# Spreading a 7-of-8 block product over four heads, two pools of PSUM banks for its parts, and an earlier fixed order

## The chip, the cores and the metric

The kernel runs on one core of one Trainium2 chip. The metric is device time in microseconds of one execution, all of it included: two layers of a transformer-like block from input in HBM to output in HBM. Less is better. Everything is computed in fp32.

## The reference

Four rows (B = 4) of 512 tokens with 512 channels. Two layers add to a residual `x`, and each branch is preceded by a gate made of a two-sided recurrence (WKV) over a side input:

```python
x = x + _L0_attn_ref(_L0_cond_ref(x, f, f, ...), ...)      # Mamba2
x = x + _L0_ffn_ref(_L0_cond2_ref(x, f, f, ...), ...)      # 8 experts, top 2
x = x + _L1_attn_ref(_L1_cond_ref(x, f, f, ...), ...)      # attention, where the change is
x = x + _L1_ffn_ref(_L1_cond2_ref(x, f, f, ...), ...)      # gated FFN
```

The attention, with 4 key groups of 4 heads each (16 heads of 128 channels):

```python
q = einsum('bsh,he->bse', x, w_q).reshape(b, 512, 4, 4, 128)
k, v = split(einsum('bsh,he->bse', x, w_kv), 2)            # one k and v for each group
scores = einsum('bqgpd,bkgd->bgqpk', q, k) * 128 ** -0.5   # causal
probs = softmax(scores)
ctx = einsum('bgqpk,bkgd->bqgpd', probs, v).reshape(b, 512, 2048)
return einsum('bse,eh->bsh', ctx, w_dense)
```

A gate is `sigmoid(x)` times a quotient of exponentially decaying sums over the tokens, forward and backward, of `exp(k)` and `exp(k) * v`. The sums depend on the side input alone, not on `x`, so gates can be made at any time before they are applied.

## The kernel before

**Stages.** Mamba2 and the first gates; the experts (37 rounds of 128 tokens each, every round three products of 8 TensorE instructions of 512 columns); attention; the gated FFN. The program is written out in Python, and a tile framework orders each engine's instructions by priority and by what is ready in its own model. Where the text says `with after(engine)`, an instruction is queued on that engine behind the last one written before it.

**Gates.** `make_gates` (L354) is a generator over pairs of channel blocks: for layer 1 there are 16 pairs, two for each of eight gates. `pump(n)` (L387) makes n larger steps of it, six to a pair, and `nudge()` (L392) one small step. After each expert round, the function `more` (L1566) calls `pump(1 + moe.i % 2)`; in attention each score block calls `nudge`. A pair is four forward scans (L259), four backward scans (L265), six products on VectorE (L276 to L280), a reciprocal by Relu, Ln and Exp on ScalarE (L316 and the lines behind it) and three last VectorE products (L322 to L333).

**Heads.** The main loop runs over `heads_`, that is (g, b, i): group, row, head. For head n it makes the queries of the next head, runs `scores` of this one, then `ahead(n)`, which makes queries, keys and values of later heads, then `settle()`, which multiplies the probabilities of three heads ago with the values (`context`), and then `dense_parts(n)`.

- `scores` (L1801): four score products `psc` (L1821) into "mm" banks, for the four blocks of 128 query tokens, each with a mask (L1824) and a row maximum (L1826) on VectorE and an exponential on ScalarE (L128). Then the probabilities are normalized, transposed in 32 x 32 blocks on VectorE (L1811), written to HBM by four DMAs on GpSimd's queue (L1850), and read back a head later as `pT` (L1868, in `collect`).
- `context` (L1873): `pctx` (L1895) into an "acc" bank; ScalarE copies it to `cx` (L1906).
- When four heads of (g, b) are through, their contexts are multiplied with the group's slice of `w_dense` and added to `x[b]`. `dense` (L1909) does it in four pieces of 8 instructions of 512 columns. `dense7` (L1930) does it as a 2 x 2 block product by Winograd's form, with seven half products in place of eight: seven `part`s of 8 instructions of 256 columns. It needs sums of weights (`dense_sums`, L1633, on GpSimd, queued by `to_sum`) and sums of contexts (L1959 to L1967, on VectorE, in place). Each part ends with two VectorE additions (L1952) to one to four blocks of `x[b]`. It is used from (1, 0) to (3, 0), nine times.
- `parts` holds the generator of the block at work; `dense_parts(n)` takes n parts of it.

**PSUM.** Eight banks: four "mm" (scores, keys, values), two "tp" (queries, transposes), two "acc" (contexts and dense parts).

**Order.** `even[0]` is true from head (0, 3, 1) to (3, 3, 1). There `in_turn()` makes TensorE run scores, contexts, queries and dense products as they are written; `scores` leaves normalizing to ScalarE (`late`, L1845) and skips one of its four nudges; and dense products are spread over the next heads. Outside it the framework orders TensorE freely, normalizing is on VectorE (L1836, L1837), and `settle` runs the whole dense product at once.

**GpSimd** also makes the sums of the query weights (`pair_weights`, L1518 to L1521), in the heads (g, 3, 0) and (g, 3, 2) of groups 1 and 2, and likewise at the end of group 0.

Of the kernel before, what the change touches and what calls it, by code (L numbers as in the profile page):

```python
# [14 lines left out]
ALU = mybir.AluOpType  # L15
# [68 lines left out]
def block_kernel(ctx: ExitStack, tc: tile.TileContext, a: dict, out: bass.AP):  # L84
# [1476 lines left out]
    with tc.tile_pool(name="moe_w2", bufs=1, reuse_waits="tile") as wm:  # L1561
# [4 lines left out]
        def more(limit):  # L1566
            while moe.i < min(limit, moe.known):
                moe.round()
                if moe.i < ALWAYS - NT + 1:
                    with after(nc.vector, nc.scalar):  # L1570
                        send()
                        pump(1 + moe.i % 2)

# [37 lines left out]
    with att as ph:  # L1611
# [318 lines left out]
        def dense7(u):  # L1930
            a11, a12, a22 = (dense_w[u.g, *v] for v in ((0, 0), (0, 1), (1, 1)))
            s1, s2, s3, s4 = dense_s[u.g]
            lo, hi = slice(0, HT), slice(HT, T)
# [3 lines left out]

            def part(w, xs, q0, q1, step=1, op=ALU.add):
                po = ps_acc("pd")
                with in_turn():  # L1940
# [12 lines left out]

            part(a11, b11, 0, 4)
            if last:
                load_dense(u.g + 1, 0, 0)
            t2 = gq.tile([P, 2, HT], F32, tag="t2", name="t2")
            for c in range(2):
                nc.vector.tensor_tensor(b11[c], b12[c], b11[c], ALU.subtract)  # L1959
                nc.vector.tensor_tensor(t2[:, c], b22[c], b11[c], ALU.subtract)  # L1960
                nc.vector.tensor_tensor(b12[c], b22[c], b12[c], ALU.subtract)
            yield True
            part(a12, b21, 0, 1)
            if last:
# [3 lines left out]
            yield True  # L1968
            part(s4, b22, 1, 2)
            yield True  # L1970
            part(s2, [t2[:, c] for c in range(2)], 1, 4)
            yield True
            part(s3, b12, 2, 4)
            if last:
                load_dense(u.g + 1, 1, 0)
            yield True
            part(a22, b21, 2, 3, op=ALU.subtract)
            if last:
                load_dense(u.g + 1, 1, 1)
                to_sum.append(u.g + 1)  # L1980
            yield True
            part(s1, b11, 1, 4, 2)
            yield None
# [4 lines left out]
        def settle():  # L1988

            old, done = held.pop(0)  # L1990
            context(old, done)
            if len(old.ctxT) == HPG:
                assert not parts
                parts.append((dense7 if seven(old) else dense)(old))
                sevens[0] = seven(old)
                if not even[0]:
                    dense_parts(NC)

        def dense_parts(n):
            while parts and n:  # L2000
                n -= 1
                if next(parts[0], None) is None:
                    parts.pop()

# [28 lines left out]
        def ahead(n):  # L2033
# [3 lines left out]
            if i % 2:  # L2037
                if heads_[n + 1 : n + 2] and heads_[n + 1] in making_q:
                    lead(n + 1)
                if n + 3 < len(heads_):  # L2040
                    lead(n + 3)
            elif n + 2 < len(heads_):
                lead(n + 2)
            s = n + 4 - i
            if i >= 2 and s < len(heads_):
                with after(nc.tensor):
# [10 lines left out]
        look_ahead(1, (0, 1))  # L2057
        groups, making_q, qs, pairs_w, parts, loading, sevens = {}, {}, {}, {}, [], [], [False]
        numbers = iter(range(GROUPS * B * HPG))
        ready, held = begin(0), []  # L2060
        for n, (g, b, i) in enumerate(heads_):
            u, qT = ready
            even[0] = (0, B - 1, 1) <= (g, b, i) < (GROUPS - 1, B - 1, 2)
            if g == 0 and i == 0 and b + 1 < B:
# [39 lines left out]
            if len(held) > 3:  # L2104
                settle()
            twice = sevens[0] and i != 2 or g == GROUPS - 1 and (b, i) >= (2, 2)
            dense_parts(2 if twice else 1)
            if (g, b, i) == (GROUPS - 1, 2, 1):
# [227 lines left out]
```

## Time and profile before

| | |
|---|---|
| time, median of 3 runs | 2237.92 us (2235.61 to 2240.21) |
| the profiled execution | 2231.51 us, span 2229.8 us, granted TensorE clock 0.979 |
| busy | PE 2101.0, DVE 1619.4, ACT 1035.7, POOL 512.0 us |
| experts with gates of layer 1 | about 744 to 1062 us |
| attention, group 0 | about 1113 to 1328 us, its last heads from 1236 |
| attention, 7-of-8 products | about 1428 to 1890 us |
| last heads | about 1890 to 1982 us, then the FFN |

Times are from one profiled execution, in us from the first instruction. PE is TensorE's multiplications, PEld its weight loads, DVE VectorE, ACT ScalarE, POOL GpSimd, SP the engine that issues most DMAs. A row of waits names the waiting engine, tile and line, then what it waited for, the sum, the number and the longest. In a row of the timeline stand start, length, engine, line, operation, tiles, shape and number, and in brackets the engine's idle time before it and what ended it. A wait for several things is put down to the last by the profile; where the named one was long done, it was another. Two rows of one tile's matmuls start one behind the other, so the distance of their starts is TensorE's cost of the first.

### The profile page before, as it was taken

Reading aid. Unit: us, or ns where it says so; the run is one execution under the profiler, and the core shown is the slowest. Engines: PE = TensorE matmul, PEld = TensorE weight load, DVE = VectorE, ACT = ScalarE, POOL = GpSimd, SP = SyncE. Lnnn points to the kernel's source line nnn. Section 1 sums busy time; section 2 is a strip of 40 time slices with the busy share of each in tenths; the row PEclk is TensorE's granted clock in tenths of the full one; section 3 lists DMA queues with packets and bytes.
Section 4 is the critical chain, followed back from the end, with each engine's and each line's share of the span. In section 5 each row is a group of like instructions: output and inputs, shape, how many; then the busy total and the mean of one; then the engine's idle time right before and its main releaser. Section 6 shows DMA issues by size and latency. Waiting matters only on the chain.

```text
span 2229.8 us, 25287 instructions
## 1 busy us (share of the span) xinstructions
PE 2101.0 (94%) x8074; PEld 1321.0 (59%) x8074; DVE 1619.4 (73%) x3026; ACT 1035.7 (46%) x2071; POOL 512.0 (23%) x684
## 2 busy tenths in 40 slices
PE   4879999999999999999988989999999999999998
PEld 2545565555665444444444546677777777568887
DVE  8699989999752566676479865788989788655332
ACT  4476676675832134333255434454545454532221
POOL 4022232422222111212233322213232223100000
PEclk9989999999999999999989999999999999999999
DMA  7542251442424458987577766666767676541100
GB/s 255 186 142 77 96 168 67 140 139 66 176 76 147 156 187 293 385 290 274 208 273 259 224 206 192 213 221 206 232 203 226 195 214 194 154 164 38 38 20 20
DMA packets 128619, 391.30 MB, mean 175 GB/s; under 512 B 15904, under 2 KB 37280, under 8 KB 117024
## 3 DMA queue, kind: packets, MB, share of 16 engines
q1 hardware_dynamic: 93088, 249.86, 32.5%
q0 software_dynamic: 33088, 135.55, 19.5%
q10 hardware_dynamic: 2304, 4.20, 0.5%
q8 instruction: 67, 1.10, 0.2%
q14 instruction: 72, 0.59, 0.1%
HBM read 363.34 MB, written 116.39 MB: 215 GB/s over the span
## 4 chain that ended last, share of the span: by engine, by line
PE 38%; DVE 7%; ACT 2%; DMA 2%; issue 1%; SPq 0%; POOL 0%; DVEq 0%; POOLq 0%; ACTq 0%
PE pctx L1895 5%; PE pq L1764 5%; PE pd L1914 4%; PE pd L1943 4%; PE psc L1821 4%; PE pv L1724 2%; PE pk L1713 2%; PE pfo L2166 2%; PE pfo L2165 2%; PE pfg L2165 2%; PE pfg L2166 2%; PE pfu L2165 2%; PE pfu L2166 2%; DMA pT<-turned 1%; PE pq L1741 1%; DVE nmax L1826 1%
## 5 line engine op out<-in xcount | busy, mean ns | idle before, releaser
L128 ACT ACTIVATE pr<-psc,nmax 128x128 f32<-128x128 f32 (+3 forms) x256 | 133.6, 524 | 286.5 <-DVE nmax L1826 285.4
L1850 POOL DMA_DIRECT2D turned<-turned x248 | 135.6, 553 | 565.8 <-DVE turned L1811 453.1
L1821 PE MATMUL psc<-kT,qT 128*128 128x128 f32 (+3 forms) x512 | 158.6, 449 | 17.6 <-ACT pr L128 17.6
L1895 PE MATMUL pctx<-pT,v 128*128 128x512 f32 (+3 forms) x512 | 152.3, 442 | 9.8 <-DMA pT<-turned 9.1
L1057 PE MATMUL pc<-h,wxb 128*128 128x512 f32 x320 | 144.0, 604 | 5.0 <-DVE h L406 4.0
L1895 PEld LDWEIGHTS pctx<-pT,v 128*128 128x128 f32 x512 | 97.3, 194 | 75.6 <-issue 53.3
L847 PE MATMUL po<-w,yT 128*128 128x512 f32 x296 | 134.1, 593 | 0.2 <-ACT yT L840 0.2
L814 PE MATMUL pg<-w,hT 128*128 128x512 f32 x296 | 133.9, 593 | 0.0
L825 PE MATMUL pn<-w,hT 128*128 128x512 f32 x296 | 133.3, 592 | 0.0
L1811 DVE STREAM_TRANSPOSE turned<-pr 128x128 f32<-128x128 f32 x248 | 119.7, 499 | 12.4 <-ACT pr L1845 6.7
L1821 PEld LDWEIGHTS psc<-kT,qT 128*128 128x128 f32 x512 | 87.7, 194 | 58.5 <-ACT pr L128 28.1
L1826 DVE TENSOR_REDUCE nmax<-psc 128x1 f32<-128x128 f32 (+3 forms) x256 | 118.4, 482 | 0.6
L1128 PE MATMUL pz<-wzt,h 128*128 128x512 f32 x256 | 116.9, 606 | 0.3 <-ACT st L1229 0.3
L1276 PE MATMUL po<-wot,yT 128*128 128x512 f32 x256 | 114.2, 600 | 0.0
L1057 PEld LDWEIGHTS pc<-h,wxb 128*128 128x128 f32 x320 | 60.6, 194 | 76.2 <-issue 71.7
L1845 ACT ACTIVATE pr<-pr,rsum 128x128 f32<-128x128 f32 x196 | 94.0, 551 | 11.9 <-DVE rsum L1843 11.9
L1764 PE MATMUL pq<-ht,wq 128*128 128x256 f32 x384 | 98.5, 379 | 0.0
L1914 PE MATMUL pd<-cx,wd 128*128 128x512 f32 x224 | 98.5, 592 | 0.0
L1952 DVE TENSOR_TENSOR xr<-xr,pd 128x256 f32<-128x256 f32 (+3 forms) x126 | 80.0, 679 | 20.7 <-PE pd L1943 20.1
L1171 ACT ACTIVATE lm<-lm,cs 128x128 f32<-128x128 f32 x256 | 81.8, 390 | 22.8 <-DMA lm<-cs 22.7
L825 PEld LDWEIGHTS pn<-w,hT 128*128 128x128 f32 x296 | 54.8, 190 | 61.7 <-issue 61.7
L814 PEld LDWEIGHTS pg<-w,hT 128*128 128x128 f32 x296 | 54.6, 190 | 60.8 <-issue 60.7
(384 smaller groups left out, 4780.7 us busy)
## 6 DMA issues: line engine op xcount, KB each, us to landing
w<-in_w1x SPq DMA_DIRECT2D x76, 1024.0 KB
turned<-turned POOLq DMA_DIRECT2D x248, 208.0 KB, 3.8
pT<-turned POOLq DMA_DIRECT2D x62, 832.0 KB, 7.4
w<-in_w2x SPq DMA_DIRECT2D x38, 1024.0 KB
wb<-in_b1x SPq DMA_DIRECT2D x38, 512.0 KB
lm<-cs SPq DMA_DIRECT2D x32, 512.0 KB
kt<-in_fT SPq DMA_DIRECT2D x62, 256.0 KB
ek<-ek SPq DMA_DIRECT2D x62, 256.0 KB
```

Source lines behind the costliest of these rows:

```text
L814: nc.tensor.matmul(pg, lhsT=hT[:, k, :], rhs=self.w1[s][0][:, k, :], start=(k == 0), stop=(k == NC - 1))
L825: nc.tensor.matmul(pn, lhsT=hT[:, k, :], rhs=self.w1[s][1][:, k, :], start=(k == 0), stop=(k == NC - 1))
L847: nc.tensor.matmul(po, lhsT=yT[:, j, :], rhs=self.w2[s][:, j, :], start=(j == 0), stop=(j == NI - 1))
L1057: nc.tensor.matmul(pc, lhsT=wxb[:, k, m * P : (m + 1) * P], rhs=h[:, k, :], start=(k == 0), stop=(k == NC - 1),)
L1764: nc.tensor.matmul(out_, lhsT=w[:, c], rhs=xs[:, c], start=(c == 0), stop=(c == 1))
L1821: nc.tensor.matmul(psc[:, :n], lhsT=qT[:, qi * P : n], rhs=u.kT[:, :n], start=True, stop=True)
L1826: nc.vector.tensor_reduce(nmax, psc[:, :n], AX.X, ALU.max, negate=True)
L1850: nc.gpsimd.dma_start(out=d[:, :, r].rearrange("c i s -> i c s"), in_=blocks[r * SQ : (r + 1) * SQ].rearrange("i c k j -> i c (k j)"),)
L1895: nc.tensor.matmul(pctx[:, kj * P :].rearrange("p (q r j) -> p q r j", r=QUAD, j=SQ), lhsT=u.v[:, kj, :], rhs=pT[:, :, 4 * kj : 10 + kj : ...
L1914: nc.tensor.matmul(po, lhsT=dense_w[u.g, m % 2, i // 2][:, i % 2, m // 2], rhs=u.ctxT[i], start=(i == 0), stop=(i == HPG - 1),)
L2165: nc.tensor.matmul(out_, lhsT=w, rhs=xs[0], start=first_, stop=False)
L2166: nc.tensor.matmul(out_, lhsT=w, rhs=xs[1], start=False, stop=last_)
```

## The change

It edits five places.

1. After an expert round `pump` makes two steps, where it made one and two in turn.
2. `dense7`: the six first context sums move from behind part a11 to ahead of part a12, a head later. Parts s4, s3 and s1 take a bank of the "mm" pool, the others stay in "acc". `to_sum` is filled after the last part, not before it.
3. `parts` may hold two blocks; the older one is worked off first.
4. How many parts follow a head: with 7-of-8 products, it was one after a block's third head (i = 2) and two after the others; from (1, 2, 0) on it is one after i = 3 and two after the others. As the first block before that takes one part in each of two heads, the last part (s1) of each block lags into the head in which the next block's a11 comes.
5. `even` is true from (0, 2, 2), three heads sooner. Guards in `ahead` keep these heads from making queries, keys and values early for group 0.

```diff
-                        pump(1 + moe.i % 2)
+                        pump(2)
...
-            def part(w, xs, q0, q1, step=1, op=ALU.add):
-                po = ps_acc("pd")
+            def part(bank, w, xs, q0, q1, step=1, op=ALU.add):
+                po = bank("pd")
...
-            part(a11, b11, 0, 4)
+            part(ps_acc, a11, b11, 0, 4)
             if last:
                 load_dense(u.g + 1, 0, 0)
+            yield True
             t2 = gq.tile([P, 2, HT], F32, tag="t2", name="t2")
             for c in range(2):
                 nc.vector.tensor_tensor(b11[c], b12[c], b11[c], ALU.subtract)
                 nc.vector.tensor_tensor(t2[:, c], b22[c], b11[c], ALU.subtract)
                 nc.vector.tensor_tensor(b12[c], b22[c], b12[c], ALU.subtract)
-            yield True
-            part(a12, b21, 0, 1)
+            part(ps_acc, a12, b21, 0, 1)
...
-            part(s4, b22, 1, 2)
+            s1, s2, s3, s4 = dense_s[u.g]
+            part(ps_mm, s4, b22, 1, 2)
             yield True
-            part(s2, [t2[:, c] for c in range(2)], 1, 4)
+            part(ps_acc, s2, [t2[:, c] for c in range(2)], 1, 4)
             yield True
-            part(s3, b12, 2, 4)
+            part(ps_mm, s3, b12, 2, 4)
...
-            part(a22, b21, 2, 3, op=ALU.subtract)
+            part(ps_acc, a22, b21, 2, 3, op=ALU.subtract)
             if last:
                 load_dense(u.g + 1, 1, 1)
+            yield True
+            part(ps_mm, s1, b11, 1, 4, 2)
+            if last:
                 to_sum.append(u.g + 1)
-            yield True
-            part(s1, b11, 1, 4, 2)
             yield None
...
-                assert not parts
                 parts.append((dense7 if seven(old) else dense)(old))
-                sevens[0] = seven(old)
...
-                    parts.pop()
+                    parts.pop(0)
...
-                if n + 3 < len(heads_):
+                if n + 3 < len(heads_) and heads_[n + 3][0]:
                     lead(n + 3)
-            elif n + 2 < len(heads_):
+            elif n + 2 < len(heads_) and heads_[n + 2][0]:
                 lead(n + 2)
             s = n + 4 - i
-            if i >= 2 and s < len(heads_):
+            if i >= 2 and s < len(heads_) and heads_[s][:2] > (0, B - 1):
...
-            even[0] = (0, B - 1, 1) <= (g, b, i) < (GROUPS - 1, B - 1, 2)
+            even[0] = (0, B - 2, 2) <= (g, b, i) < (GROUPS - 1, B - 1, 2)
...
-            twice = sevens[0] and i != 2 or g == GROUPS - 1 and (b, i) >= (2, 2)
-            dense_parts(2 if twice else 1)
+            if (1, 2, 0) <= (g, b, i) < (GROUPS - 1, 2, 2):
+                dense_parts(1 if i == 3 else 2)
+            else:
+                dense_parts(3 if (g, b, i) == (GROUPS - 1, 2, 2) else 2 if g == GROUPS - 1 and b >= 2 else 1)
```

More of the change, by code (lines that the diff above doesn't have):

```diff
@@ L1931, in dense7 @@
             a11, a12, a22 = (dense_w[u.g, *v] for v in ((0, 0), (0, 1), (1, 1)))
-            s1, s2, s3, s4 = dense_s[u.g]
             lo, hi = slice(0, HT), slice(HT, T)
@@ L2057, in block_kernel @@
         look_ahead(1, (0, 1))
-        groups, making_q, qs, pairs_w, parts, loading, sevens = {}, {}, {}, {}, [], [], [False]
+        groups, making_q, qs, pairs_w, parts, loading = {}, {}, {}, {}, [], []
         numbers = iter(range(GROUPS * B * HPG))
```

## The prediction

> **What bounds the kernel now.** I read the page first, then busy time by stage, then TensorE's waits stage by stage, then single moments in the timeline.
>
> From the page, the share of each engine, and the group of VectorE additions that empty the product's banks:
>
> ```profile
> PE 2101.0 (94%) x8074; PEld 1321.0 (59%) x8074; DVE 1619.4 (73%) x3026; ACT 1035.7 (46%) x2071; POOL 512.0 (23%) x684
> ...
> L1952 DVE TENSOR_TENSOR xr<-xr,pd 128x256 f32<-128x256 f32 (+3 forms) x126 | 80.0, 679 | 20.7 <-PE pd L1943 20.1
> ```
>
> TensorE is the bound. The change removes no matmul, so it can only win TensorE's idle time. Busy time by stage (stretch, length, PE, PEld, DVE, ACT, POOL, granted clock, DMA share, GB/s):
>
> ```profile
> 744.00:1062.00 318.00, 312.77 (x910) 149.91 (x909) 210.62 (x307) 111.78 (x155) 60.89 (x54) 1.00 0.75 266
> ...
> 1236.00:1328.00 92.00, 84.00 (x267) 45.63 (x266) 70.72 (x154) 39.31 (x89) 30.32 (x46) 0.94 0.66 213
> ...
> 1428.00:1890.00 462.00, 449.37 (x1973) 340.87 (x1972) 397.90 (x890) 221.81 (x557) 125.50 (x211) 1.00 0.67 211
> 1890.00:1982.00 92.00, 87.49 (x294) 49.85 (x293) 48.08 (x117) 37.85 (x88) 11.46 (x21) 0.98 0.58 189
> ```
>
> The four stages that the change touches: experts (5.2 us idle), the last heads of group 0 (8.0), the heads with 7-of-8 products (12.6), the last heads (4.5): 30.4 us is the ceiling, plus matmuls slowed after a wait. VectorE is at 86% in the third stage (397.9 of 462) and at 66% among the experts.
>
> TensorE's waits in the 7-of-8 stage, whole:
>
> ```profile
> PE pv L1724 <- ACT pr L128: 4.6, 3, 2.3
> PE pd L1943 <- ACT cx L1906: 4.4, 5, 1.7
> PE pctx L1895 <- DMA pT<-turned: 3.6, 2, 2.0
> ```
>
> In group 0's last heads and in the last heads of all, the timeline shows one wait each that matters, both on TensorE:
>
> ```profile
> 1320.76 4.50 PE L1895 MATMUL pctx<-pT,v 128*128 128x512 f32 x8 [5.59 <-DMA pT<-turned]
> ```
>
> ```profile
> 1935.38 0.49 PE L1821 MATMUL psc<-kT,qT 128*128 128x128 f32 x2 [2.55 <-ACT pr L128]
> ```
>
> The same context product takes 2.32 us elsewhere and 4.50 here: 2.2 us more at a low granted clock (0.94 over the stage), so this one wait costs 7.8.
>
> **The change part by part.**
>
> *Second bank pool.* Within a head, the context product takes one of two "acc" banks, the first part the other, and the second part must wait until ScalarE has copied the context away. That is the 4.4 us row: five such waits out of 27 heads with two parts. With one part of each pair in an "mm" bank, nothing waits for that copy. Against it: the mm bank must be free again for the next head's fourth score product. After the mm part come the acc part (8 matmuls of 0.216 = 1.7 us) and three score products (1.3 us): 3.0 us of cover. The additions take 2 x 0.68 = 1.4 us at most, and the page's row has VectorE waiting for the part (20.1 us), not behind it, in 21 of 63 parts. Where VectorE lags by over 1.6 us the rest is paid, and the exponentials queue behind it. In the 1515.8 case it lagged by 1 us. I take -4 (between -4.4 and +3, 27 heads by 0.1).
>
> *Order of parts and sums.* A finished block's four heads had 1, 2, 2, 2 parts; now, with the last one lagging into the next block, 2, 1, 2, 2. The third head (with the key product, 3.4 us) grows from 12.1 to 13.8 us of TensorE, the fourth (with the value product, 3.6 us) shrinks by 1.7. TensorE's total is unchanged. The eight 0.42 us subtractions now come a head after the part whose operands they overwrite, so VectorE's 17.0 us of idle before them (waiting for that part) goes. This is what made scores late before the value product: subtractions (2.5 us) and two 1.2 us additions stood ahead of the first masks. But the worst of it is GpSimd:
>
> ```profile
> 1639.68 3.30 DVE L1959 TENSOR_TENSOR cx<-cx 128x256 f32<-128x256 f32 x1 [1.58 <-PE pd L1943]
> ...
> 1643.35 2.35 DVE L1952 TENSOR_TENSOR xr<-xr,pd 128x1024 f32<-128x1024 f32 x2
> ```
>
> A subtraction of 0.42 us takes 3.30 while three weight sums of 1.28 us run on GpSimd. `to_sum` moves one head later too, so for groups 2 and 3 both sides move together and meet again, only group 1 comes free (its weight sums stay). What waits for it then is the s4 part, some 1.3 us later in its head than the value product. The waits of 4.6 us become about 2.5: -2 (bounds -4.6, +2).
>
> Here a rule speaks against the change. The Trainium skill ("SBUF — State Buffer", Who interferes with whom) says that a VectorE instruction with two SBUF inputs fully blocks behind a GpSimd instruction that reads SBUF. The 3.30 us row agrees. By that rule the subtractions of block 1, now at the start of head (g, 3, 0), meet the query weights' sums there; blocked in full in both groups, the sum below would be 3.4 us smaller, -8.1 in place of -11.5.
>
> By rows: the query sums run 0.73 + 0.72 + 0.72 us from 1507.13, 0.9 us after that head's scores begin, and already stretched a scan from 1.2 to 2.3 us. In two places this puts up to 2.2 us on VectorE, whose transposes feed the context two heads on, just where the 3.6 us row waits (1524.98 and 1727.86): I take +1 (bounds -3.6, +4.4).
>
> *Fixed order three heads sooner.* From (0, 2, 2) the scores, contexts, queries and product go to TensorE as written, normalizing moves to ScalarE, and the product of block (0, 1) is spread over four heads. Now it runs in one piece, 1282.6 to 1296.3, between the third and fourth score product of head (0, 2, 3), so that head's transposes end only at 1301, GpSimd writes them then, does three query sums, and reads pT at 1314.6: the 5.59 us wait. Spread, that softmax ends some 10 us sooner and 3.4 us parts lie between. In (1, 3, 1), where this spreading already holds, the same spot waits 1.7. So 7.8 becomes about 2: -5.5. What it may cost: scores (0, 2, 2) queue behind the context (0, 1, 2), scores (0, 2, 3) behind the keys, values and queries of row 3. Before, row 3's keys began at 1269.6, ahead of those scores, so the order is nearly the same. At worst two new waits of 5.6: bounds -7.8, +6. ScalarE takes 1.9 us more in each of three heads, at 43% load.
>
> *Two gate steps after each expert round.* Steps per round go from 1.5 to 2 in some 28 rounds: 14 steps. Gate pairs end every 44.6 us there, four rounds, six steps: 2.3 pairs more. Each is about 17.8 us of VectorE (four scans of 1.21, four of 1.27, six ops of 0.69, three of 1.2) and 8 of ScalarE. VectorE's load there goes from 66% to 79%. The load DMAs (six of 256 KB per pair, on SP's queue among the expert weights) add 4% to a stage whose DMA share is 0.75; counting packets against issues, the 1 MB weight loads land 1.4 to 7.6 us after issue and are used some 16 us after it, so I cost that at nothing; if the cover is gone each late load stalls a round by its lateness. What can hurt is ScalarE: a pair's reciprocal (1.15 + 1.15 + 1.06 us, two table loads of 1.28) stands before the next tanh:
>
> ```profile
> 799.66 0.63 PE L838 MATMUL pyt<-ident,u 128*128 128x128 f32 x4 [1.41 <-DVE u L832]
> ```
>
> Two of the six pairs there cost 1.4 us so. With 8 or 9 pairs at another phase: 3 or 4 of them, and routing's 2.0 us wait a little longer: +2 (bounds -3 if none, +10 if all).
>
> What this buys: pairs take some 90 us each in attention (the last four end at 1685, 1777, 1868 and 1940), so the last one ends some 210 us sooner, about 1730. The 2.55 us wait above, with 0.79 and 0.47 beside it, stands behind that pair's reciprocal on ScalarE (1933.83, 1935.21). Of 3.8 us: -3 (bounds -3.8, 0).
>
> *At nothing:* the guards in `ahead` keep group 0 from making queries early, as before; `load_dense` stays with its parts (one of four pieces comes a head later, still several heads ahead of use); the GpSimd weight sums (4 x 1.27 us) come one head later, as does their reader.
>
> Sum: -4 - 2 + 1 - 5.5 + 2 - 3 = -11.5, say -12. The profiled execution took 2231.51 (span 2229.8): 2219.5. The median of the three runs, 2237.92, lies 6.4 above it; with the same gain, 2226.
>
> **The rivals.**
>
> *Waits only move (15%).* The bank wait becomes a wait of the fourth score product, the pT chain binds again: only half of group 0's gain and the end remain, about -5: 2233. For: VectorE stays at 86%. Against: it waits for the parts.
>
> *Fixed order stalls (10%).* Two more waits of 5.6 in the three heads eat the rest: -12 + 5.5 + 6 = about 0: 2238. For: 5.59 was seen in the first fixed heads. Against: it had a bulk product ahead of it.
>
> *Slower: the experts pay (15%).* ScalarE and VectorE come late for each round's tanh. Each such round costs 1.4 us; beyond 9 rounds (12 / 1.4) above today's two the gain is gone, and 20 of 28 give +25 - 12: 2251. For: 79% VectorE, in-order. Against: rounds with two steps exist already, 14 of them, and from 879 to 1058 TensorE has no wait.
>
> *Chain gains as summed: 60%.*
>
> **How the numbers follow.** About 0.2% (4.5 us) can be told from no change. Faster: 0.60 and half of the first rival, 0.68. Same: the other half and half of the second, 0.13. Slower: the rest, 0.19. The low end adds 12 us to the gain (all pv and pctx waits gone, no new expert stall): 2214. The high end takes in the second rival and part of the third, leaving out some 10%: 2245.
>
> **What would show it.** Right: in the 7-of-8 stage no pd wait for cx; the 5.59 us wait at 2 or less; no gate operation after about 1750 and the last psc waits gone; gate scans denser among the experts with TensorE's waits there under 8 us; block (0, 1)'s product in four pieces. Wrong: psc waiting for pd's additions, new waits before queries in (0, 2, 3), or many pyt waits before 1062.

## The result and the profile after

The changed kernel took 2250.28 us (median of 7 runs, 2243.01 to 2253.60), the kernel before 2237.92 beside it: ratio 1.0055 (95% interval 1.0039 to 1.0071), so about 12 us slower. The forecast was 2226 us, in a range from 2214 to 2245: wrong in sign and out of the range. The profiled execution took 2251.86 us (span 2249.9, clock 0.970). It lies 20.1 us above the profiled span before: that execution lay 6.4 us below its median and the one after 1.6 above.

Lines of changed code have moved: `part` multiplies at L1942 and adds at L1951. The page after, the engines' shares and the additions that empty the product's banks:

```profile
PE 2120.3 (94%) x8074; PEld 1333.3 (59%) x8074; DVE 1605.4 (71%) x3005; ACT 1051.3 (47%) x2089; POOL 516.8 (23%) x684
...
L1951 DVE TENSOR_TENSOR xr<-xr,pd 128x256 f32<-128x256 f32 (+3 forms) x126 | 80.2, 678 | 51.9 <-PE pd L1942 51.8
```

VectorE now waits 51.8 us for parts in place of 20.1: the additions did come free of what stood ahead of them. TensorE's idle time is no smaller (129.6 us of the span after, 128.8 before). By stretches, each from the start of one matmul to that of another:

| stretch | before | after | measured | forecast |
|---|---|---|---|---|
| start to expert round 6 (nothing edited) | 744.0 | 747.1 | +3.1 | 0 |
| rounds 6 to 10, with the second routing | 50.7 | 57.0 | +6.3 | +2 with the next |
| round 10 to the first keys (pk) | 318.9 | 329.8 | +10.9 | |
| first keys to the first score product of (0, 2, 0) | 124.5 | 128.8 | +4.3 | 0 |
| on to the first of (0, 3, 3) | 104.2 | 99.6 | -4.6 | -5.5 |
| on to the first of (1, 1, 2) | 86.4 | 86.4 | 0 | 0 |
| on to the first of (3, 2, 2), the "7-of-8 stage" below | 454.0 | 450.2 | -3.8 | -5 |
| on to the FFN, "the end" below | 99.5 | 103.2 | +3.7 | -3 |
| FFN | 247.6 | 247.9 | +0.3 | 0 |

(124.5 and 128.8 are each two stretches added. The expectations name the marks of the 7-of-8 stage as third scores; its length is the same.) A length is that of one profiled execution. Over the runs, the stretch before round 6, which nobody edited, took 744.0 to 751.9 us, and rounds 6 to 10 with the old steps 50.7 or 52.4. Of the -3.8, 1.7 is the lagging part of the last block: its 8 matmuls run behind (3, 2, 2) now and are in the +3.7.

The loss lies mostly where two gate steps follow a round. The +4.3 behind it comes with the steps too (+6.1 with the steps alone, -0.6 with all the rest of the change). It is not idle time (TensorE idled 15.2 us there, 16.7 before): the granted clock was lower, 0.88 from the first score product on where it was 0.92 before. What lowered it was not taken apart. Busy time of three of the changed stages after (experts, last heads of group 0, 7-of-8 products; same columns as before):

```profile
747.00:1084.00 337.00, 320.26 (x914) 153.01 (x913) 243.19 (x345) 135.44 (x182) 63.39 (x55) 0.98 0.74 269
1262.00:1348.00 86.00, 79.84 (x262) 45.01 (x261) 59.53 (x131) 44.58 (x99) 29.47 (x46) 0.96 0.69 220
1448.00:1906.00 458.00, 448.26 (x1964) 341.12 (x1963) 373.50 (x868) 214.59 (x548) 125.71 (x211) 0.99 0.65 206
```

Among the experts VectorE rose to 72% (243.19 of 337), not to 79%, and TensorE idled 16.7 of 337 us. Its waits there, all of them:

```profile
PE po L847 <- ACT yT L840: 4.5, 4, 1.5
PE ptok L606 <- DVE os L600: 4.4, 1, 4.4
PE pyt L838 <- DVE u L832: 4.0, 2, 2.4
PE pg L814 <- DMA w<-in_w1x: 2.7, 3, 1.5
PE pidx L691 <- DVE of L688: 0.6, 1, 0.6
PE pn L825 <- DMA w<-in_w1x: 0.4, 1, 0.4
```

They sum to 16.6 us; before there were three rows (pyt 2.8, pidx 2.0, ptok 0.4; 5.2 us). The waits cost more than their length: taking each matmul's distance to the next start, less that of an undisturbed one of its shape (0.429 us for 512 columns), the excess from round 6 to the first keys went from 12.5 to 29.6 us. These 17.1 us are the two stretches' +17.2. What comes on top of the waits is a lower clock behind the two longest: behind the 4.42 us of ptok the granted clock was 0.50 from 766 to 770 us, behind a 2.42 us wait of pyt 0.50 from 833.4 to 836.4. Behind the 1.51 us of po at 1029.95 it stayed at 1.00.

How each arises is seen in the timeline. First, at the second routing, VectorE's queue holds gate scans between the routing's rows ov and os, and TensorE's product of them waits:

```profile
761.67 1.20 DVE L259 TENSOR_TENSOR_SCAN den<-decay,ek 128x512 f32<-128x512 f32 x1
762.79 0.66 DVE L598 TENSOR_TENSOR ov<-lane,q 128x512 f32<-128x512 f32 x1
763.37 1.27 DVE L265 TENSOR_TENSOR_SCAN num<-decay,num,f 128x511 f32<-128x511 f32 x1
...
765.88 2.08 PE L606 MATMUL ptok<-os,ov 128*128 128x128 f32 x8 [4.42 <-DVE os L600]
```

Second, ScalarE stands at a gate's f for a scan of VectorE; the copy yT is next in its queue:

```profile
1028.70 0.72 ACT L261 ACTIVATE f<-den,fall 128x511 f32<-128x511 f32 x1 [2.10 <-DVE num L265]
1029.32 0.58 ACT L840 ACTIVATE yT<-pyt 128x512 f32<-128x512 f32 x1
...
1029.95 2.84 PE L847 MATMUL po<-w,yT 128*128 128x512 f32 x6 [1.51 <-ACT yT L840]
```

This comes once in a gate pair, every 35.3 us (959, 995, 1030, 1065): two steps after each of three rounds make a pair, and it repeats at the same place. The Trainium skill ("Perfetto Trace Analysis", Tensor Engine Instruction) calls ScalarE and VectorE strict first-in first-out; the two rows above show it, with yT starting 0.62 us after an f that idled 2.10 us.

Third, SP. Its queue's waits (SPq) at the load of the second bias b2 (L759), which may start only when VectorE's addition o has read the old one; before, then after:

```profile
SPq L759 <- DVE o L852: 29.5, 19, 4.1
```

```profile
SPq L759 <- DVE o L852: 58.0, 16, 6.6
```

Behind it in SP's queue stand the next first halves of w1, for which pg waits. These are weights that I had costed at nothing.

### The profile page after: what moved, and what is told of

It is laid out like the page before. It is cut to its first block, busy times and chain, and to the rows that moved or that the text cites. A ratio compares the mean times of both kernels' runs of the same rounds, so it can differ in the third digit from the quotient of the medians.

```text
span 2249.9 us, 25245 instructions
## 1 busy us (share of the span) xinstructions
PE 2120.3 (94%) x8074; PEld 1333.3 (59%) x8074; DVE 1605.4 (71%) x3005; ACT 1051.3 (47%) x2089; POOL 516.8 (23%) x684
## 5 line engine op out<-in xcount | busy, mean ns | idle before, releaser
L1821 PE MATMUL psc<-kT,qT 128*128 128x128 f32 (+3 forms) x512 | 157.1, 446 | 11.6 <-ACT pr L128 10.4
L1951 DVE TENSOR_TENSOR xr<-xr,pd 128x256 f32<-128x256 f32 (+3 forms) x126 | 80.2, 678 | 51.9 <-PE pd L1942 51.8
L1845 ACT ACTIVATE pr<-pr,rsum 128x128 f32<-128x128 f32 x208 | 99.8, 550 | 17.2 <-DVE rsum L1843 17.2
L853 POOL DMA_INDIRECT rows_o<-o,idx_o x37 | 41.5, 1121 | 257.8 <-DVE o L852 232.7
```

The costliest lines, as they stand in the source:

```text
L1821: nc.tensor.matmul(psc[:, :n], lhsT=qT[:, qi * P : n], rhs=u.kT[:, :n], start=True, stop=True)
```

## Experiments among the experts

Ratios are to the kernel before, measured beside each, with 95% intervals; "way" is from round 6 to the first keys (369.6 us before, 386.8 after, of one profiled execution each).

**The changed kernel with the old steps.**

```diff
-                        pump(2)
+                        pump(1 + moe.i % 2)
```

> The changed kernel with the gate steps after an expert round as before (one and two in turn). Theory A (the two gate steps after each expert round cost the time, the attention's edits about balance): the experts' stretch is back at its old length, so some 14 to 17 us less than the changed kernel, 2233 to 2238 us, 0 to 5 below the kernel before. Theory B (the attention's edits cost it: lagging part, shared banks, earlier order): it stays within 4 us of the changed kernel, about 2248.

2232.58 us, ratio 0.9983 (0.9970 to 0.9996), way 369.6 us. As theory A has it: all else in the change wins about 4 us, and on top of it the steps cost 0.72%, 16 us.

**The steps alone**, in the kernel before:

```diff
-                        pump(1 + moe.i % 2)
+                        pump(2)
```

> The kernel before with two gate steps after each expert round and nothing else. Theory A: 12 to 17 us slower than the kernel before, 2250 to 2255 us, with the same waits among the experts as in the changed kernel (pyt for DVE, po for the ACT copy yT, ptok for DVE). It may win 2 to 4 us back in the last heads, where no gate operation is left on ScalarE. Theory B: within 3 us of the kernel before.

2246.15 us, ratio 1.0032 (1.0015 to 1.0049), about 7 us slower. The way is theory A's, 384.3 us (+14.7), but the time is not, which it put 12 to 17 us up: the 7-of-8 stage took 446.4 us (-7.6), and the end 101.0 (+1.5). So the attention gains from the steps where the forecast had nothing. The waits of TensorE that shrink in that stage are those for pv (4.6 us before, 2.1 here) and pd (4.4 and 2.1), the same that the banks and the order of the change aim at; beside these the steps win 1.0 us there (450.2 in the changed kernel, 451.2 with the old steps). Whether the sooner end of the gates wins or the places at which their operations meet the heads was not tested: in the kernels of this section with the changed attention the stage took 447.9 to 455.2 us. Both experiments say that the steps turn the gain into a loss; they cost 7 us alone and 16 us in the changed kernel.

**Two steps only behind the routing.**

```diff
-                        pump(2)
+                        pump(2 if moe.i > 10 else 1 + moe.i % 2)
```

> The changed kernel, but with two gate steps after a round only from round 11 on; up to there one and two in turn, as before the change. Between the products of rounds 6 and 10, where the second routing is made, the changed kernel took 57.1 us and the kernel before 50.7. Theory A (gate scans in VectorE's queue ahead of the routing's one-hot rows make TensorE wait, 4.4 us at ptok): this stretch returns to about 50.7 us, the stretch behind it (329.8 us) stays within 2 us of that, and the kernel takes about 2244 us. Rival B (the same number of steps is paid wherever it is put): the stretch behind grows by what the first wins, and the time stays at about 2250 us.

2242.11 us, ratio 1.0016 (0.9997 to 1.0035). Rounds 6 to 10 took 50.7 us: theory A, 6.3 us for the scans in the routing. Not foreseen: the rest also fell, from 329.8 to 323.9. Steps are a fixed sequence, so fewer of them early on shift which operation meets which round; that this is the reason was not shown.

**The product by fall on VectorE.**

```diff
-            nc.scalar.mul(f[:, : T - 1], s[:, : T - 1], fl[i])
+            if in_experts[0]:
+                nc.vector.tensor_scalar(f[:, : T - 1], s[:, : T - 1], fl[i], None, ALU.mult)
+            else:
+                nc.scalar.mul(f[:, : T - 1], s[:, : T - 1], fl[i])
```

> The changed kernel, but among the experts the gates' multiplication by fall (f, L261, 0.72 us each on ScalarE, four to a pair) is done by VectorE. Theory A (ScalarE's queue: f waits there for a scan of VectorE, and the copy yT that TensorE needs stands behind it): TensorE's waits of po for yT (4.5 us in four rows, and 1.67 us each by distance of starts) vanish, and the stretch from round 10 to the first keys shrinks from 329.8 to about 323; about 2244 us. Rival B (VectorE's load sets the cost): four more operations of some 0.4 us for each of 8 or 9 pairs go onto VectorE, waits of pyt for u grow by as much, and the time is 2250 us or more.

2252.89 us, ratio 1.0074 (1.0046 to 1.0101), way 390.4 us. The yT waits fell to 1.2 us, so what held them is shown, but nothing was won. The weights' wait, from TensorE's waits in this kernel:

```profile
PE pg L817 <- DMA w<-in_w1x: 6.9, 4, 2.4
```

VectorE's o came still later (SP waited 64.9 us for it). So rival B's time came, and the load on VectorE is the likely reason, though by SP's queue more than by pyt (4.8 us, 4.0 in the changed kernel).

**The second bias a round later.**

```diff
-            nc.sync.dma_start(out=self.b2[s], in_=a["b2x"][e].partition_broadcast(P), **kw)
+            self.b2_due.append((s, e, kw))
...
                     self.weights(i + 1)
+                self.load_b2()
```

> The changed kernel (two gate steps after every round), but the load of the second bias (b2, L759) is queued on SP a round later, behind the next weights' loads. In the changed kernel SP waits 58 us in 16 rows at that load for VectorE's addition o (29.5 us before the change), and the first halves of w1 are queued behind it. Theory A (VectorE's late addition holds SP's queue, and the weights come late): TensorE's waits of pg and pn for w (3.1 us in four rows) vanish, those for yT, u and os stay, and the stretch from round 10 to the first keys falls from 329.8 to about 326; about 2247 us. Rival B (the weights are late for the gates' own loads or for the DMA share of 0.74): the waits stay within 1 us.

2242.97 us, ratio 1.0024 (1.0001 to 1.0047), way 381.2 us (-5.6). SP's wait for o fell to 7.6 us, the weights' waits from 3.1 to 1.9. The stretch behind the routing came to 324.5, better than theory A's 326; the waits for yT (3.2) and u (2.2) are shorter too, so not all of the 5.6 us is the weights'.

**Both of these.**

> As the last one, and the gates' multiplication by fall among the experts on VectorE. That alone cut the waits of po for yT from 4.5 to 1.2 us, but those of pg and pn for w grew from 3.1 to 7.8, and the stretch took 332.9 us. Theory A (two queues, each with its own head: ScalarE's and SP's): with both mended the stretch falls to 322 to 325 us and the time to about 2244. Rival B (VectorE has too much to do): waits of pyt for u take their place, and the stretch stays at 329 us or more.

2242.22 us, ratio 1.0021 (1.0000 to 1.0043), way 383.3 us (stretch 326.6). Between the theories: weights 1.5 us, yT 2.2, but pyt for u 5.9. With SP's queue mended, work on VectorE is paid at the next place.

**No table loads.** This kernel leaves out the logarithm and the exponential of the reciprocals among the experts, so its gates have other values.

```diff
-        act(flat(r), flat(r), AF.Ln, bias=tiny[:, 0:1])
+        act(flat(r), flat(r), AF.Tanh if in_experts[0] and l >= 2 else AF.Ln, bias=tiny[:, 0:1])
```

> The changed kernel, but a gate pair of layer 1 whose reciprocal is made among the experts takes Tanh in place of Ln and of the Exp behind it: as many operations on ScalarE of the same size, but no table loads (two of 1.28 us for each pair). The gates of those pairs come out as other values. Theory A (the block of a reciprocal with its two table loads, 5.9 us, stands before the next tanh): TensorE's waits of pyt for u (4.0 us) fall to 1 us or less, those of po for yT stay, and the time falls by 3 to 4 us to about 2247. Rival B (head of the queue: what waits is what stands behind an operation that waits itself, not behind the reciprocal): no more than 1 us changes.

2242.52 us, ratio 1.0032 (1.0008 to 1.0056), way 380.4 us (-6.4). pyt's waits fell to 0.8 us: the reciprocal's block delays tanh as the forecast said. The yT waits fell too (to 2.5), against the expectation, so the 6.4 us are not the block's alone.

**Three edits together**: two steps behind the routing only, the later bias, no tables (so here too the gates have other values).

> The changed kernel with three edits at once: two gate steps only after the rounds from 11 on, the second bias loaded a round later, and Tanh in place of Ln and Exp in the reciprocals made among the experts (the gates of those pairs come out as other values). Alone they shortened the way from round 6 to the first keys (386.9 us; 369.6 before the change) by 12.3, 5.6 and 6.5 us. Theory A (three queues, each with its own late operation, make the whole loss among the experts: VectorE's at the routing, SP's at the bias, ScalarE's at the reciprocal): the way comes to 369 to 372 us and the time to about 2234 us, ratio 0.999. Rival B (the steps themselves cost, each through VectorE, wherever the queues are mended): 375 us or more, and 2240 us.

2238.46 us, ratio 1.0009 (0.9992 to 1.0025), way 371.3 us, as theory A has it; the time is 4 us above its figure, between the two theories. All of TensorE's waits in the experts that are left:

```profile
PE po L856 <- ACT yT L849: 3.5, 4, 0.9
PE pidx L694 <- DVE of L691: 2.0, 1, 2.0
PE ptok L609 <- DVE ov L602: 0.4, 1, 0.4
```

Alone the three won 12.2, 5.6 and 6.4 us, together 15.5. They do not add up: with the first two alone (the kernel with two steps further down) the way is 374.6, no shorter than with the first. So the routing's 6.3 us is a cost of its own; the remaining 11 us hang on how gate operations meet the rounds, through SP's, ScalarE's and VectorE's queues, and cannot be split among them.

## Experiments in attention

Here all kernels but the very last have the old gate steps; the base is the first experiment (ratio 0.9983, 7-of-8 stage 451.2 us, end 102.1). Every kernel with a lagging part has 1.7 us less work in that stage than the kernel before, and 1.7 us more in the end. How much chance and edits elsewhere move this stage: three of the kernels below have the same code in it and took 440.7, 443.6 and 443.3 us.

**Fixed order where it was.**

```diff
-            even[0] = (0, B - 2, 2) <= (g, b, i) < (GROUPS - 1, B - 1, 2)
+            even[0] = (0, B - 1, 1) <= (g, b, i) < (GROUPS - 1, B - 1, 2)
```

> The changed kernel with the old gate steps and the fixed order from (0, 3, 1) as before: what is left of the change is the spreading of the 7-of-8 parts, their sums and banks. If the earlier order is worth nothing (the pT wait of 5.6 us gone, a new wait of 4.9 us for the queries behind pcb in its place), the time equals the one with the earlier order within 2 us. If it costs, this one is 3 to 6 us faster; if it gains, 3 to 6 us slower. The 5.6 us wait of pctx near 1320 us should be back, the pcb wait of 4.9 us gone.

2235.81 us, ratio 0.9994 (0.9979 to 1.0009). The stretch from (0, 2, 0) to (0, 3, 3) goes back from 100.8 to 104.8, and the 5.5 us wait for pT is back: the earlier order is worth 4.0 us there. In the time it is 3.2 us, with intervals that overlap. Banks, parts and sums alone, all that this kernel differs in otherwise, are worth 0.06%, 1.3 us, not told from nothing: the 7-of-8 stage is 2.6 us shorter, the end 2.4 longer, and 1.7 of each is the part that now lags.

**All parts in acc banks.**

```diff
-            part(ps_mm, s4, b22, 1, 2)
+            part(ps_acc, s4, b22, 1, 2)
```

(and likewise s3 and s1)

> The changed kernel with the old gate steps and all seven parts in the acc banks. If the mm banks did what the forecast said, the pd waits for the copy cx are back: about 4 us in the 7-of-8 heads, and the time is 3 to 4 us longer than with the mm banks. If they only moved waits to pctx and psc, those fall by as much and the time is the same within 2 us.

2233.29 us, ratio 0.9983 (0.9966 to 1.0000): the time does not tell the second pool's worth from nothing, as the expectation had it if waits only move. In the profiled executions the stage is 2.9 us longer without it (454.1) and the end 1.6 shorter (100.5). Waits of pd for cx are back, but pctx waits less (7.1 us, 10.4 in the base), and psc does not wait for VectorE's additions (2.1 us in the base). Waits of TensorE in the 7-of-8 stage, changed kernel, then this one:

```profile
PE pctx L1895 <- ACT pr L128: 4.1, 2, 3.4
PE pctx L1895 <- DMA pT<-turned: 2.6, 1, 2.6
PE pctx L1895 <- ACT pr L1845: 2.4, 1, 2.4
PE psc L1821 <- DVE xr L1951: 0.6, 2, 0.4
```

```profile
PE pd L1942 <- ACT cx L1906: 6.5, 5, 3.3
PE pctx L1895 <- DMA pT<-turned: 3.6, 2, 3.4
PE pctx L1895 <- ACT pr L128: 3.5, 1, 3.5
```

The pd rows are gone from the changed kernel, as forecast, and pctx has 9.1 us in place of the 3.6 of the kernel before. The named ScalarE operations are not what pctx reads. It reads pT, and GpSimd's queue shows why that is late (changed kernel; the same pattern stands 12 us earlier in the base):

```profile
1667.51 0.56 POOL L1850 DMA_DIRECT2D turned<-turned  x1 [11.64 <-DVE turned L1811]
1668.08 1.28 POOL L1637 TENSOR_TENSOR ws<-ws,wd 128x512 f32<-128x512 f32 x1
1669.30 1.27 POOL L1639 TENSOR_TENSOR wd<-wd,wd 128x512 f32<-128x512 f32 x1
1670.53 1.27 POOL L1638 TENSOR_TENSOR ws<-wd,ws 128x512 f32<-128x512 f32 x1
1671.74 0.56 POOL L1868 DMA_DIRECT2D pT<-turned  x1
...
1677.48 1.19 PE L1895 MATMUL pctx<-pT,v 128*128 128x512 f32 x1 [3.43 <-ACT pr L128]
```

Three sums of product weights (`to_sum`, one head later than before) stand ahead of the read of pT; pctx starts 5.7 us after that read is issued, having waited 3.4. The sums' own 3.7 us are not all that holds the read. Elsewhere it is issued right behind the writes of the head before (here 1653.0), while in this queue a first write of the next head stands ahead of it too, for which GpSimd waited 11.64 us. The kernel before had the same order in its queue, but in a head with a value product, so that 10.7 us lay between the read and its product, and nothing waited for it:

```profile
1642.62 0.56 POOL L1868 DMA_DIRECT2D pT<-turned  x1
...
1653.29 2.32 PE L1895 MATMUL pctx<-pT,v 128*128 128x512 f32 x8
```

Three experiments move these sums.

**Sums behind the scores.**

```diff
-            while to_sum:
-                dense_sums(to_sum.pop())
...
             prs = scores(u, i, qT)
+            while to_sum:
+                dense_sums(to_sum.pop())
```

> The changed kernel with one and two gate steps in turn (2232.6 us when run before), and with the four sums of product weights on GpSimd (1.27 us each) queued behind the scores of their head, and so behind its writes of the turned probabilities and its read of pT, in place of ahead of them. Theory A (three of these sums stand ahead of a read of pT in two heads; the read lands 5.7 to 5.9 us after its issue, when TensorE has already waited 3.3 and 3.6 us): both waits of pctx (1665.6 and 1864.6 us in that kernel) vanish, and the 7-of-8 stage from the third score of (1, 1, 2) to that of (3, 2, 2) falls from 451.2 to about 445; about 2226 us. Rival B (the read is late for the transposes on VectorE in any case): the waits stay, within 1 us, and the time is 2232 us.

2248.80 us, ratio 1.0054 (1.0035 to 1.0073). The two waits of pctx are gone, and part s4, the sums' reader, waits instead:

```profile
PE pd L1942 <- POOL ws L1638: 15.9, 2, 8.1
```

Neither theory had this. Behind the writes, three of the sums run only from 1671.5 us on, and s4, in the same head, starts at 1675.2; in the kernel before their sums were through 14.5 us ahead of s4. The stage took 466.7 us.

**Sums between the read and the writes.**

```diff
                 if qi == 0:
                     collect(1)
+                    while to_sum:
+                        dense_sums(to_sum.pop())
```

(and not at the head's start)

> The changed kernel with one and two gate steps in turn (ratio to the kernel before 0.9983), its four sums of product weights on GpSimd queued behind the read of the last head's pT and ahead of this head's writes. Queued ahead of that read they cost two waits of pctx (3.3 and 3.6 us), queued behind the writes two waits of the s4 part of 8.2 and 8.0 us. Theory A (only GpSimd's order around the read decides): neither wait is there, the 7-of-8 stage from the third score of (1, 1, 2) to that of (3, 2, 2) falls from 451.2 to 444 to 446 us, and the kernel takes about 2227 us, ratio 0.995 to 0.996. Rival B (the sums are one head too late: the reader s4 stands in the same head): pd waits for ws 1 to 4 us in both heads, the stage stays at 448 to 453 us.

2227.01 us, ratio 0.9958 (0.9940 to 0.9976): theory A's time. Neither wait is left; the stage took 447.5 us, 1.5 over the theory's, with one pctx wait of 4.0 and one pv wait of 1.9 at other heads, and psc waits 4.4 us for VectorE's additions.

**Parts s4 and s1 exchanged**, so that three of the sums can be made a head sooner:

```diff
-            part(ps_mm, s4, b22, 1, 2)
+            part(ps_mm, s1, b11, 1, 4, 2)
...
-            part(ps_mm, s1, b11, 1, 4, 2)
-            if last:
-                to_sum.append(u.g + 1)
+                to_sum.append((dense_sums, u.g + 1))
+            yield True
+            part(ps_mm, dense_s[u.g][3], b22, 1, 2)
+            if last:
+                to_sum.append((dense_sum4, u.g + 1))
```

> The changed kernel with one and two gate steps in turn, with parts s4 and s1 exchanged in order, so that s4 is the part that lags into the next block. Then three of the four weight sums no longer need its end and are queued a head sooner, as before the change; only the sum for s4 comes in the later head, and its reader is the last of the next block's parts. Theory A (the sums in the head of their reader are what costs; one head sooner they have room): no wait of pctx behind sums, no wait of pd for ws, 7-of-8 stage 444 to 447 us, about 2228 us. Rival B (in any head three sums of 1.27 us stand ahead of some read of pT): a pctx wait of 3 us or more one head sooner in both groups, stage about 451 us, 2232 us.

2223.09 us, ratio 0.9948 (0.9925 to 0.9971), stage 440.7 us: better than theory A's 444. TensorE's waits there:

```profile
PE psc L1825 <- DVE xr L1955: 3.3, 4, 1.8
PE pctx L1899 <- ACT pr L128: 1.7, 1, 1.7
PE pctx L1899 <- DMA pT<-turned: 0.6, 1, 0.6
```

No wait for a sum. But the second pool has its price here: all of psc's waits are fourth score products that wait until VectorE's additions have freed their "mm" bank, just the cost that the forecast named against it. Still the stage is 13.3 us under the kernel before, 11.6 without the part that lags out of it, where the forecast had 5.

**Row 3's sums sooner.** In the fixed order the changed kernel has a new wait (5.4 us in the last kernel):

```profile
1283.18 1.97 PE L1543 MATMUL pcb<-ident,rr 128*128 128x128 f32 x8 [4.92 <-DVE rr L1538]
```

The transposes pcb of row 3 are now written ahead of everything else and nothing may pass them. On top of the last kernel:

```diff
+            if (g, b, i) == (0, B - 2, 1):
+                combine(b + 1, (2, 3))
             prs = scores(u, i, qT)
-            if g == 0 and i == 1 and b + 1 < B:
+            if g == 0 and i == 1 and b + 2 < B:
```

> The kernel with s4 as the lagging part, and for row 3 the second half of the experts' sums (L1537 and L1538, then pcb) made ahead of the scores of head (0, 2, 1), not behind them. With the earlier fixed order TensorE waits 5.4 us at that pcb (1263.97 us in that kernel, 4.9 us in the changed one), since nothing else may go ahead of it. Theory A (the price of the earlier order is this one wait): it vanishes, the stretch from the first score of (0, 2, 0) to the last of (0, 3, 3) comes, together with the one before it, 4 to 5 us lower, and the time falls to about 2219 us. Rival B (the two loads land late, or the sums now hold ScalarE's exponentials of (0, 2, 1)): 2 us at most, or a loss.

2220.56 us, ratio 0.9924 (0.9906 to 0.9943). The wait is gone; from (0, 2, 0) to (0, 3, 3) takes 97.0 us in place of 100.8, the stretch before it 123.8 in place of 124.7: 4.7 together, though keys now wait 3.1 us. In the measured time the step is smaller (0.13% against the next kernel, which ran beside it), and the intervals overlap. It has the lowest time of all, below both the kernel before and the changed one.

**Gates sooner, once more.** The kernel with s4 last and the later bias, with the old steps and with two behind the routing:

```diff
-                        pump(1 + moe.i % 2)
+                        pump(2 if moe.i > 10 else 1 + moe.i % 2)
```

> The kernel with s4 as the lagging part, one and two gate steps in turn, and only the second bias loaded a round later. Theory A (SP's queue is late only when VectorE is, with two steps after every round): experts as before, 318.9 us from round 10 to the first keys, 2223 us. Rival B (the bias holds the weights back with fewer steps too): 1 to 2 us less.

> The kernel with s4 as the lagging part (2223.1 us, ratio 0.9948, one and two gate steps in turn) with the second bias loaded a round later and two gate steps after the rounds from 11 on. Theory A (gates ended sooner are worth 4 us or more in the 7-of-8 stage and the last heads, as in the kernel before with two steps, 7.6 us; the experts pay 2 to 4 us): 2221 us, at best 2218. Rival B (with the waits on the read of pT gone, the gate steps in attention stand in the way of nothing): stages behind 1430 us unchanged, only the experts' price is left: 2225 to 2227 us.

Old steps: 2224.13 us, 0.9937 (0.9919 to 0.9956), way 373.3 us: the later bias wins nothing there, which fits theory A's time, though the way is 3.7 us longer than without it (1.7 of that, in rounds 6 to 10, also stands in the kernel with the sums between the read and the writes, which has nothing edited there). Two steps behind the routing: 2230.41 us, 0.9981 (0.9963 to 0.9998), way 374.6 us, the 7-of-8 stage 446.5 us against 443.6, the end 101.9 against 101.0. Rival B, and worse: gates that end sooner won nothing here. The medians are 6 us apart, 10 by the ratios; the profiled runs account for 2, and the rest stays open.

## Why the forecast was wrong, step by step

- **Two gate steps, +2, late weights at nothing, the routing a little longer: the step that failed.** It measured +17.2 us, and its upper bound was +10; the stretch behind, put at 0, took another 4.3. The form was that of the rival "the experts pay", but only in part its mechanism: tanh behind the reciprocal is 4.0 us of waits at two moments, beside 4.4 for the routing's os, 4.5 for yT behind a gate's f on ScalarE and 3.1 for weights. That the rival's example came to 2251 us, nearly the time measured, is luck. I took the phases of 14 rounds with two steps as those of 28 and priced only the wait that the trace before showed. That pattern was one and two in turn; with two in every round the operations meet the rounds elsewhere. The price of "a little longer" should have been bounded by what a step can put on VectorE ahead of os (two scans of 1.2 and two of 1.27 us); that of the weights by SP's queue: it waited 29.5 us for VectorE's o before the change already, and I did not price that row.
- **Last heads, -3.** Gates did end sooner (last product at 1782, 1940 before; about 1730 was forecast), and psc's waits for ACT pr fell from 3.8 to 1.4 us. But 1.7 us of the lagging part came into this stretch and pctx waits 2.1 for pT: +3.7 in the changed kernel. With the old steps and the changed parts it is already +2.6, so the gates add 1.1 there and win nothing.
- **Bank pool, -4.** The mechanism was right (no pd wait for cx), the gain not told from nothing: the first rival, "waits only move", in both forms that it gave. The chain of pT took over in the changed kernel, and fourth score products wait for VectorE's additions, 0.6 us there, 2.1 in the base, 3.3 with s4 last.
- **Order of parts and sums, -2, +1.** The weight sums did "come one head later, as does their reader"; what failed is their price, nothing. In the later head there is no value product, and the read of pT behind the sums has 5.7 us before its product in place of 10.7. Ahead of pT's read they cost 3.4 and 2.4 us in waits in the changed kernel, behind the writes 8 us each. With s4 last the stage falls by 10.5 us against the base; TensorE's waits there fall from 12.5 to 5.6 us, and I have not traced the rest. The subtractions did meet the weight sums again, as forecast; the one that meets them most is now the last of the four:

```profile
L1966 DVE TENSOR_TENSOR cx<-t,cx 128x256 f32<-128x256 f32 x18 | 13.0, 724 | 14.5 <-PE pd L1942 14.5
```

  All 72 subtractions take 36.9 us after and 36.8 before. VectorE's 17.0 us of idle time ahead of the first of them became 2.8, but the 4.8 ahead of the last became the 14.5 above, so most of it only moved. The rule of the Trainium skill's "SBUF — State Buffer" (Who interferes with whom) still agrees with the rows: the worst subtraction, at 1668.91, took 3.18 us beside three weight sums. The query weights' sums stretched one subtraction by more than 0.3 us (from 0.42 to 1.66, at 1725.77 beside L1519 and L1520), nearer to the +1 than to the full blocking in both groups.
- **Fixed order, -5.5.** Measured -4.6 in the changed kernel and -4.0 by experiment, and 3.8 to 4.7 more once the new wait for rr is gone. The pctx wait fell from 5.59 to 1.24 us as foreseen; the wait of pcb was in no bound by name, but in size within the two of 5.6 that I had set as the worst.

So the attention part was of the right sign (ratio 0.9983, about -4 of the -10.5 that its terms, without the gates', sum to), and an edit of one line turned it round.

## What to carry to other kernels

Cost an instruction that is added in front of a queue by who stands behind it on every queue that its operands touch: here a VectorE scan delayed a ScalarE copy, and a late VectorE addition held a bias load on SP, and with it weights for the next round. When work on a queue is moved, look at what stands behind it in its new place, and how much time that has until it is needed; and take a periodic pattern's stall count only for that very pattern. What a fixed order wins it can lose at the one instruction that must now go first.

## What was not expected of the hardware

A wait's cost can be its length and more: from 1677.4 to 1683.0, behind a wait of 3.43 us, the granted clock was 0.50, and the first matmul of 512 columns took 0.98 us to the next start against 0.43. Among the experts, waits that grew by 11.4 us lengthened the work by 17.2. A wait's length alone does not decide it: in the changed kernel the clock stayed at 1.00 behind a wait of 2.41 us (1881.88) and was 0.50 behind one of 2.07 (1957.00). What decides was not tested. On GpSimd's queue, the product that waited for a read of pT began 5.7 and 6.3 us after the read's issue. And of three edits that won 5 to 12 us alone, two together won no more than the better one.
